# A step size finished in its PSUM bank: one more reader for the bank, one fewer SBUF input for VectorE

## The chip, the cores and the metric

The kernel runs on one core of one Trainium2 chip. The metric is the device time of the launch in microseconds (us), the median of three runs, and lower is better. The core has five engines that each work through their own queue in order: PE (TensorE, matrix multiply), DVE (VectorE), ACT (ScalarE), POOL (GpSimd) and SP (SyncE, which here only issues transfers). Sixteen DMA engines move data between the device memory and the on-chip memory SBUF. Matrix products land in PSUM, a small memory of eight banks; one bank holds 128x512 fp32 values.

## The reference

Four layers work on images of 96 channels and 64x64 pixels, four images in a batch. Layer 0 is a state-space layer: it normalises, projects and convolves the image to an input `u` of 192 channels, and then runs a recurrence over the 4096 pixels, in four directions `k` (by rows and by columns, each forward and back). Layer 1 is a deformable convolution, layer 2 a Fourier mixer with a feed-forward part, layer 3 linear attention with a feed-forward part. Only the input of the recurrence of layer 0 matters for the change:

```python
delta = jax.nn.softplus(dts + delta_bias[None, :, :, None])
def step(h, inp):
    d_t, u_t, b_t, c_t = inp
    dA = jnp.exp(d_t[..., None] * A)
    h = dA * h + (d_t * u_t)[..., None] * b_t[:, :, None, :]
    y = jnp.einsum('bkdn,bkn->bkd', h, c_t)
    return (h, y)
```

The kernel needs the step size `delta` itself (for `dA`) and its product with the convolved input, `delta * u`.

## The kernel before

**The scan.** `Layer0.scan` runs over 1,536 units. A unit is one image, one direction, one of four stretches of 1,024 pixels and eight channels, whose 16 states make 128 partitions. For each unit ScalarE turns the step size into the decay (L1014), TensorE spreads `delta * u` over the states into a PSUM pair `db` (L1020), VectorE multiplies that by the input weights (L1034) and runs the recurrence (L1042), GpSimd multiplies by the output weights (L1051) and TensorE sums the states (L1070). The step sizes come from device memory into `da` tiles, a ring of twelve, with transfers that ScalarE's queue issues (L993).

**Beside the scan** two streams of filler work run. One (`ends`) prepares layer 0 of the next images and then runs layers 2 and 3; the other (`middle`) finishes layer 0 and runs layer 1. All of this is one program: a planner decides while the program is written. Each piece of filler is a generator that yields steps with a planned cost for each engine (`cost(pe=.., dve=.., act=.., pool=..)`), and `pipe` interleaves several such chains (here five, at least two steps apart). A step is put into the program when the planner's clock has room on its engines and the step before it is planned to be over. At the end the program order is fixed for every engine (`in_program_order`).

**Banks.** While the scan runs, all filler shares three PSUM banks (`net.mm`). `holds=1` in a step says that the chain keeps a bank after that step, and a new chain starts only where fewer than three are held. `takes` and `frees` count the tiles of small rings in the same manner.

**The chain that is changed** is `Layer0.steps`, which runs 192 times: six times for each chunk of 512 pixels of each image. A chain covers 128 channels of one direction, or the remaining 64 channels of two. In order it does this:

- TensorE projects into the bank `pd` (L840); ScalarE computes four functions from it (L842 to L846: `ex`, `lw`, `w1`).
- VectorE forms a correction in `w1` (L849), GpSimd subtracts it from `lw` (L851).
- VectorE finishes the step size, `rl = max(pd, 0) + lw`, from PSUM into SBUF (L853), and the bank is free.
- VectorE multiplies `rl` by the convolved input `xa` or `xc`, into `ex`. The four forms are L859 and L860 (halves of 64 partitions), L866 (the input read by columns) and L872.
- SP writes `rl` to device memory (L875, `de`), from where L993 reads it.
- ScalarE and TensorE split `ex` into three bf16 parts (L879 to L889) in another bank, `pr`, and SP writes those out (L894).

L853 and the multiply are two steps of the planner, with a planned VectorE cost of 0.7 us each.

Of the kernel before, what the change touches and what calls it, by code (L numbers as in the profile page):

```python
# [15 lines left out]
ALU = mybir.AluOpType  # L16
# [3 lines left out]
B, C, H, W = 4, 96, 64, 64  # L20
# [162 lines left out]
def cost(pe=0.0, dve=0.0, act=0.0, pool=0.0, **more):  # L183
    return Step((pe, dve, act, pool), **more)


def wait(us=0.0, **more):

    return Step((0.0,) * 4, us, **more)
# [75 lines left out]
class Chain:  # L265
    def __init__(self, steps, ready):
        self.steps, self.ready = steps, ready
        self.done, self.holds, self.new, self.takes = 0, 0, True, []
        self.kind = steps.gi_code


def pipe(net, chains, width, every=0, lane=None, **tiles):
# [5 lines left out]
    while True:  # L278
        if more and len(active) < width:
            steps = next(chains, None)  # L280
            if steps is None:
                more = False
            else:
                active.append(Chain(steps, clock.now()))
                continue
# [269 lines left out]
class Layer0:  # L555
# [267 lines left out]
    def steps(self, b, ks, j, us, dtw, sm, xdbl):  # L823

        net = self.net
        nc = net.nc
        cs = slice(j * CH, (j + 1) * CH)
        tk = f"{b}_{j}_" + "".join(str(k) for k in ks)
        both = len(ks) == 2

        def tile_of(name, bufs):
            return sm.tile([128, CH], F32, name=f"{name}{tk}", tag=name, bufs=bufs)

        yield wait(new=True, takes="ex lw")


        pd = net.mm(f"pd{tk}")
        for i, k in enumerate(ks):
            o, m = (pd[64 * i : 64 * i + 64], slice(128, DI)) if both else (pd, slice(0, 128))
            nc.tensor.matmul(o, lhsT=dtw[:, k, m], rhs=xdbl[k % 2, j], start=True, stop=True)  # L840
        ex = tile_of("ex", 3)
        nc.scalar.activation(ex, pd, AF.Abs)  # L842
        nc.scalar.activation(ex, ex, AF.Exp, scale=-1.0)
        lw, w1 = tile_of("lw", 2), tile_of("w1", 2)
        nc.scalar.activation(lw, ex, AF.Ln, bias=net.one)
        nc.scalar.activation(w1, ex, AF.Identity, bias=net.one)  # L846
        yield cost(pe=2.2 if both else 1.1, act=2.7, holds=1, takes="rl")
        rl = tile_of("rl", 2)
        nc.vector.scalar_tensor_tensor(w1, w1, -1.0, ex, ALU.add, ALU.subtract)  # L849
        yield cost(dve=0.7, holds=1)  # L850
        nc.gpsimd.tensor_sub(lw, lw, w1)  # L851
        yield cost(pool=1.3, holds=1)
        nc.vector.scalar_tensor_tensor(rl, pd, 0.0, lw, ALU.max, ALU.add)  # L853
        yield cost(dve=0.7, frees="lw")
        if both and ks[0] % 2 == ks[1] % 2:
            q, xc = ks[0] % 2, us[2]
            own, far = slice(64 * q, 64 * q + 64), slice(64 - 64 * q, 128 - 64 * q)
            turned = xc.rearrange("p (a b) -> p b a", a=64)
            nc.vector.tensor_mul(ex[own], rl[own], xc[own, cs])  # L859
            nc.vector.tensor_mul(  # L860
                ex[far].rearrange("p (a b) -> p a b", b=64),
                rl[far].rearrange("p (a b) -> p a b", b=64),
                turned[far, j * NR : (j + 1) * NR, :],
            )
        elif not both and ks[0] % 2:
            nc.vector.tensor_mul(  # L866
                ex.rearrange("p (w h) -> p w h", h=H),
                rl.rearrange("p (w h) -> p w h", h=H),
                us[1][:, j * NR : (j + 1) * NR, :],
            )  # L870
        else:
            nc.vector.tensor_mul(ex, rl, us[2 if both else 0][:, cs])  # L872
        parts = ((0, 64, ks[0], 128), (64, 128, ks[1], 128)) if both else ((0, 128, ks[0], 0),)
        for p0, p1, k, c0 in parts:
            nc.sync.dma_start(self.de_d[b][k][c0 : c0 + p1 - p0, cs], rl[p0:p1])  # L875
        yield cost(dve=0.7, takes="du", frees="rl")

        du = sm.tile([128, 3, CH], BF16, name=f"du{tk}", tag="du", bufs=2)
        nc.scalar.copy(du[:, 0, :], ex)  # L879
        yield cost(act=0.6, new=True)  # L880
        pr = net.mm(f"pr{tk}")
        nc.tensor.matmul(pr, lhsT=net.ident, rhs=ex, start=True, stop=False)  # L882
        nc.tensor.matmul(pr, lhsT=self.minus, rhs=du[:, 0, :], start=False, stop=True)
        nc.scalar.copy(du[:, 1, :], pr)
        yield cost(pe=1.5, act=0.6, holds=1, frees="ex")
        nc.tensor.matmul(
            pr, lhsT=self.minus, rhs=du[:, 1, :], start=False, stop=True, skip_group_check=True
        )
        nc.scalar.copy(du[:, 2, :], pr)  # L889
        yield cost(pe=0.4, act=0.6)  # L890
        for p0, p1, k, c0 in parts:
            for p in range(p0, p1, 32):
                dst = self.du_d[b][k, j, (c0 + p - p0) // 32].rearrange("(s c) t -> c s t", s=3)
                nc.sync.dma_start(dst, du[p : p + 32])  # L894
        self.ready.update((b, k, both, j) for k in ks)
        yield wait(frees="du")
# [1044 lines left out]
```

## Time and profile before

| | |
|---|---|
| median of three runs | 8476.31 us (8467.26 to 8499.47) |
| the profiled execution | 8455.38 us, span 8453.6 us |
| VectorE busy | 6826.4 us, 81% of the span |
| TensorE busy | 6424.4 us, 76% |
| GpSimd busy | 5621.2 us, 66% |
| ScalarE busy | 4914.8 us, 58% |
| scan and its multiply, VectorE (L1042, L1034) | 3578.1 and 1865.4 us |
| last chain of step sizes (L889) | starts at 4549.7 us |
| last GpSimd multiply of the scan (L1051) | starts at 7418.8 us |

The busy times of the engines overlap, so they don't add up to the span. A wait that the profile names is read as "instruction that waited <- what ended the wait". The chain of waits is followed back from the last instruction, at each step to what released it. An instruction off this chain can take longer without moving the end, up to some slack that the chain does not show.

### The profile page before, as it was taken

Reading aid. Unit: us, or ns where it says so; the run is one execution under the profiler, and the core shown is the slowest. Engines: PE = TensorE matmul, PEld = TensorE weight load, DVE = VectorE, ACT = ScalarE, POOL = GpSimd, SP = SyncE. Lnnn points to the kernel's source line nnn. Section 1 sums busy time; section 2 is a strip of 40 time slices with the busy share of each in tenths; the row PEclk is TensorE's granted clock in tenths of the full one; section 3 lists DMA queues with packets and bytes.
Section 4 is the critical chain, followed back from the end, with each engine's and each line's share of the span. In section 5 each row is a group of like instructions: output and inputs, shape, how many; then the busy total and the mean of one; then the engine's idle time right before and its main releaser. Section 6 shows DMA issues by size and latency. Waiting matters only on the chain.

```text
span 8453.6 us, 96209 instructions
## 1 busy us (share of the span) xinstructions
PE 6424.4 (76%) x31848; PEld 2772.6 (33%) x31848; DVE 6826.4 (81%) x5122; ACT 4914.8 (58%) x8979; POOL 5621.2 (66%) x4308
## 2 busy tenths in 40 slices
PE   6765787678766777977767889777788777797587
PEld 2211221112222223321222555222455232464273
DVE  2799889987789898779888898898898988838714
ACT  5665566555567777855566677645576876333224
POOL 1566566665568888856578898766798997627700
PEclk8776787678767778977667898786798787898698
DMA  3676678877679888877788999776899897744410
GB/s 98 169 209 186 166 190 214 204 186 188 171 205 241 233 235 220 230 187 198 194 216 233 236 237 245 184 177 175 224 239 235 216 228 188 187 111 138 142 60 17
DMA packets 773926, 1608.27 MB, mean 190 GB/s; under 512 B 264082, under 2 KB 355758, under 8 KB 771223
## 3 DMA queue, kind: packets, MB, share of 16 engines
q10 hardware_dynamic: 244224, 843.17, 39.2%
q1 hardware_dynamic: 455478, 532.37, 24.4%
q0 software_dynamic: 73728, 226.57, 10.1%
q8 instruction: 256, 4.19, 0.2%
q14 instruction: 240, 1.96, 0.1%
HBM read 1345.43 MB, written 256.29 MB: 189 GB/s over the span
## 4 chain that ended last, share of the span: by engine, by line
PE 32%; DVE 26%; DMA 12%; POOL 11%; issue 9%; ACT 8%; SPq 2%; ACTq 1%; DVEq 0%; POOLq 0%
DVE da L1042 12%; POOL da L1051 7%; DVE db L1034 7%; PE pc L763 3%; DMA da<-de 3%; PE py L1070 3%; PE ps L1416 3%; PE f L1510 3%; POOL g L1383 3%; PE pd L1432 2%; PE db L1020 2%; ACT g L1395 2%; ACT da L1014 2%; DMA du<-du 1%; PE h L1551 1%
## 5 line engine op out<-in xcount | busy, mean ns | idle before, releaser
L1051 POOL TENSOR_TENSOR da<-da,bc 128x1024 f32<-128x1024 f32 x1536 | 3664.1, 2387 | 351.6 <-DVE da L1042 233.3
L1042 DVE TENSOR_TENSOR_SCAN da<-da,st,db 128x1024 f32<-128x1024 f32 x1152 | 2701.1, 2345 | 124.1 <-ACT da L1014 12.8
L1034 DVE TENSOR_TENSOR db<-db,bc 128x1024 f32<-128x1024 f32 x1536 | 1865.4, 1214 | 614.7 <-PE db L1020 613.1
L1014 ACT ACTIVATE da<-da,w_al 128x1024 f32<-128x1024 f32 x1536 | 1737.7, 1146 | 405.7 <-DMA da<-de 166.9
L1383 POOL DMA_INDIRECT g<-table,idx x1152 | 1206.8, 1048 | 360.2 <-issue 178.7
L1020 PE MATMUL db<-du,rep 24*128 24x512 bf16 x3072 | 683.7, 450 | 774.4 <-DVE da L1042 729.0
L1070 PE MATMUL py<-da,w_fold 128*32 128x512 f32 x6144 | 1091.8, 784 | 43.6 <-issue 25.2
L1395 ACT ACTIVATE g<-g,wt 128x96 f32<-128x96 f32 x3456 | 964.0, 365 | 107.1 <-DMA g<-table,idx 18.4
L1042 DVE TENSOR_TENSOR_SCAN da<-da,db 128x1024 f32<-128x1024 f32 x384 | 877.0, 2284 | 54.7 <-ACT da L1014 19.6
L1416 PE MATMUL ps<-w_ident,g 128*96 128x128 f32 x3744 | 680.7, 325 | 252.3 <-issue 107.6
L1020 PEld LDWEIGHTS <-rep 24*128 24x128 bf16 x3072 | 147.3, 93 | 1839.2 <-DVE da L1042 1164.6
L851 POOL TENSOR_TENSOR lw<-lw,w 128x512 f32<-128x512 f32 x192 | 244.0, 1271 | 700.5 <-DVE w L849 667.8
L1416 PEld LDWEIGHTS ps<-w_ident,g 128*96 128x96 f32 x3744 | 483.5, 144 | 601.3 <-issue 178.9
L1049 POOL COPY st<-da 128x1 f32<-128x1 f32 x1152 | 232.2, 202 | 674.1 <-DVE da L1042 655.8
L763 PE MATMUL pc<-pad,wc 96*128 96x512 f32 x1152 | 576.3, 636 | 7.0 <-DVE rl L853 5.3
L1424 ACT COPY st<-ps 96x384 f32<-96x384 f32 x384 | 180.2, 472 | 572.3 <-PE ps L1416 533.8
L882 PE MATMUL pr<-ex,w_ident 128*128 128x512 f32 x384 | 311.2, 904 | 125.5 <-DVE ex L866 53.5
L1432 PE MATMUL pd<-st,wdc 96*128 96x256 f32 x1152 | 323.7, 434 | 12.7 <-DVE rl L853 6.0
L763 PEld LDWEIGHTS pc<-pad,wc 96*128 96x128 f32 x1152 | 217.9, 200 | 318.6 <-issue 303.5
L840 PE MATMUL pd<-xd,w_dtw 103*64 103x512 f32 (+1 forms) x512 | 273.4, 799 | 47.0 <-DVE rl L853 15.6
L1070 PEld LDWEIGHTS py<-da,w_fold 128*32 128x32 f32 x6144 | 158.1, 124 | 381.1 <-issue 300.3
L1432 PEld LDWEIGHTS pd<-st,wdc 96*128 96x128 f32 x1152 | 243.2, 219 | 104.2 <-issue 39.5
(259 smaller groups left out, 8631.4 us busy)
## 6 DMA issues: line engine op xcount, KB each, us to landing
da<-de ACTq DMA_DIRECT2D x1536, 512.0 KB
du<-du SPq DMA_DIRECT2D x1536, 96.0 KB
bc<-bcd SPq DMA_DIRECT2D x128, 512.0 KB
y<-yb SPq DMA_DIRECT2D x384, 128.0 KB
de<-rl SPq DMA_DIRECT2D x128, 256.0 KB
m<-in_dft SPq DMA_DIRECT2D x128, 256.0 KB
ad<-y ACTq DMA_DIRECT2D x192, 128.0 KB
table<-pix SPq DMA_DIRECT2D x256, 96.0 KB
```

Of the source, the lines that this page charges most:

```text
L763: nc.tensor.matmul(pp, lhsT=wc[:, q, g * 128 : (g + 1) * 128], rhs=pad[:, r0 + dy : r0 + dy + NR, dx : dx + W], start=(q == 0), stop=(q == 8),
L882: nc.tensor.matmul(pr, lhsT=net.ident, rhs=ex, start=True, stop=False)
L1014: self.net.nc.scalar.activation(u.da, u.da, AF.Exp, scale=self.al[:, a : a + 1])
L1020: self.net.nc.tensor.matmul(db[:, h, :], lhsT=self.rep[64 * u.q + 32 * h : 64 * u.q + 32 * h + 24], rhs=u.du[64 * u.q + 32 * h : 64 * u.q ...
L1034: self.net.nc.vector.tensor_mul(u.db, u.db, u.bc[:, 0, :])
L1042: nc.vector.tensor_tensor_scan(u.along(u.hh), u.along(u.da), u.along(u.db), first, ALU.mult, ALU.add)
L1051: self.net.nc.gpsimd.tensor_mul(u.hh, u.hh, u.bc[:, 1, :])
L1070: nc.tensor.matmul(py[p0 : p0 + 32], lhsT=self.fold[:, u.i, :], rhs=hc[:, h * CH : (h + 1) * CH], start=u.sums["add"] is None and u.i == 0 ...
L1383: nc.gpsimd.indirect_dma_start(out=g[:, k, :], out_offset=None, in_=self.tables[b % 2], in_offset=bass.IndirectOffsetOnAxis(ap=idx[:, n : ...
L1395: nc.scalar.activation(pixel, pixel, AF.Identity, scale=wt[:, n, c : c + 1])
L1416: nc.tensor.matmul(pt[:, k, :], lhsT=g[:, k, c * C : (c + 1) * C], rhs=net.ident, is_transpose=True, start=(c == 0), stop=(c == corners - 1),)
L1432: nc.tensor.matmul(po, lhsT=wdc[:, k, :], rhs=st[:, k, :], start=(k == 0), stop=(k == 8))
```

## The change

VectorE now writes the finished step size back into `pd` in place, and the multiply reads it from there. ScalarE then copies `pd` to `rl`, and SP's transfer of `rl` follows the copy. For the planner the two VectorE instructions are one step of 1.4 us, the bank is held through the copy, the copy is a step of 0.6 us on ScalarE, and an empty step follows the transfer. The tile `rl` is made just ahead of the copy. Nothing else in the program differs; the ring `da` has twelve tiles in both.

```diff
         yield cost(pe=2.2 if both else 1.1, act=2.7, holds=1, takes="rl")
-        rl = tile_of("rl", 2)
         nc.vector.scalar_tensor_tensor(w1, w1, -1.0, ex, ALU.add, ALU.subtract)
         yield cost(dve=0.7, holds=1)
         nc.gpsimd.tensor_sub(lw, lw, w1)
         yield cost(pool=1.3, holds=1)
-        nc.vector.scalar_tensor_tensor(rl, pd, 0.0, lw, ALU.max, ALU.add)
-        yield cost(dve=0.7, frees="lw")
+        nc.vector.scalar_tensor_tensor(pd, pd, 0.0, lw, ALU.max, ALU.add)
         if both and ks[0] % 2 == ks[1] % 2:
             q, xc = ks[0] % 2, us[2]
...
-            nc.vector.tensor_mul(ex[own], rl[own], xc[own, cs])
+            nc.vector.tensor_mul(ex[own], pd[own], xc[own, cs])
             nc.vector.tensor_mul(
                 ex[far].rearrange("p (a b) -> p a b", b=64),
-                rl[far].rearrange("p (a b) -> p a b", b=64),
+                pd[far].rearrange("p (a b) -> p a b", b=64),
...
         elif not both and ks[0] % 2:
             nc.vector.tensor_mul(
                 ex.rearrange("p (w h) -> p w h", h=H),
-                rl.rearrange("p (w h) -> p w h", h=H),
+                pd.rearrange("p (w h) -> p w h", h=H),
...
         else:
-            nc.vector.tensor_mul(ex, rl, us[2 if both else 0][:, cs])
+            nc.vector.tensor_mul(ex, pd, us[2 if both else 0][:, cs])
+        yield cost(dve=1.4, holds=1, frees="lw")
+        rl = tile_of("rl", 2)
+        nc.scalar.copy(rl, pd)
+        yield cost(act=0.6)
         parts = ((0, 64, ks[0], 128), (64, 128, ks[1], 128)) if both else ((0, 128, ks[0], 0),)
         for p0, p1, k, c0 in parts:
             nc.sync.dma_start(self.de_d[b][k][c0 : c0 + p1 - p0, cs], rl[p0:p1])
-        yield cost(dve=0.7, takes="du", frees="rl")
+        yield wait(takes="du", frees="rl")
```

## The prediction

> **What bounds the kernel now.** I read the page's busy shares first, then the windows by stage, the rows of the tiles that change, the waits, and last the chain of waits, which prices each step. The page gives VectorE the largest load, but a chain that changes engine all the time:
>
> ```profile
> PE 6424.4 (76%) x31848; PEld 2772.6 (33%) x31848; DVE 6826.4 (81%) x5122; ACT 4914.8 (58%) x8979; POOL 5621.2 (66%) x4308
> PE 32%; DVE 26%; DMA 12%; POOL 11%; issue 9%; ACT 8%; SPq 2%; ACTq 1%; DVEq 0%; POOLq 0%
> ```
>
> The windows split the span at the last step-size instruction (4540 us), the last scan (7415) and the end of layer 1 (8030):
>
> ```profile
> 182.00:4540.00 4358.00, 3199.78 (x11203) 1016.37 (x11201) 3770.88 (x2615) 2720.84 (x4470) 2936.29 (x2205) 0.76 0.78 203
> 4540.00:7415.00 2875.00, 2309.32 (x14702) 1172.76 (x14702) 2504.63 (x1681) 1795.41 (x3796) 2296.39 (x1775) 0.82 0.86 213
> 7415.00:8030.00 615.00, 441.39 (x2661) 286.03 (x2662) 383.27 (x537) 169.29 (x337) 372.03 (x312) 0.80 0.47 132
> ```
>
> Columns are us, then PE, PEld, DVE, ACT, POOL busy. In the first stage, the only one that runs the changed code, VectorE is busy 3771 of 4358 us (87%), TensorE 73%, GpSimd 67%, ScalarE 62%. Of VectorE's 587 idle us the largest item is 342.9 us in 189 waits for TensorE's L1020, that is, for a TensorE queue that is itself stuck. So no engine bounds the stage alone: VectorE is nearest, and TensorE holds it up.
>
> The rows that change, from the view of tile ex (ns: min/median/max) and, as yardstick, a multiply with one PSUM input (L1613):
>
> ```profile
> L872 DVE TENSOR_TENSOR ex<-rl,xa x64: 680/692/5254, 113.7 to 4537.8; 128x512 f32<-128x512 f32 x64
> L866 DVE TENSOR_TENSOR ex<-rl,xa x64: 1025/1071/3171, 513.8 to 4464.4; 128x512 f32<-128x512 f32 x64
> L872 DVE TENSOR_TENSOR ex<-rl,xc x48: 668/692/4834, 1218.1 to 4495.8; 128x512 f32<-128x512 f32 x48
> L1613 DVE TENSOR_TENSOR tl<-tl,lnb x64: 655/677/684, 4636.9 to 8373.2; 96x512 f32<-96x512 f32 x64
> ```
>
> The minimum of L872 is that of L1613, but its maximum is over seven times its median. The same instruction is sometimes blocked for up to 4.6 us. L866 reads xa by columns and costs 1.03 us even unblocked.
>
> [...] two SBUF inputs reach 5254 ns, one SBUF and one PSUM input never passes 684. [...]
>
> **Part by part**
>
> *Multiplies (L859, L860, L866, L872).* By the groups view they are busy 81.0+53.2 (L872), 102.9 (L866), 26.7 (L860) and 19.7 (L859), 283.5 us in all. With one PSUM input I price them unblocked: 112×0.677 + 64×1.071 + 16×1.042 + 16×0.677 = 172. VectorE loses 112 us of work. How much of it moves the end? The chain's pieces in order of time hold 52.3 (L872, 46 pieces), 50.0 (L866, 35), 20.4 (L860) and 12.4 (L859), 135 us; the saved fraction is 112/283.5 = 0.39, so **−53 us** on the path. Bounds: nothing, to −112 if VectorE alone sets the pace.
>
> *Step size in place (L853).* PSUM in place instead of SBUF out: 678 ns now; the in-place PSUM multiply L1034 is 1208 for 1024 columns[...]. No change. It also stops waiting for the transfer de<-rl (11.2 us, 2 waits); the copy inherits that, so I count 0.
>
> *Copies.* 192 new ScalarE copies, PSUM to SBUF, 128x512; the nearest row, L1081 yb<-py, has a mean of 570 ns: 109 us on ScalarE. Its busy time is on the chain in 8/58 of cases: **+15 us**. Bounds 0 and +109. Queued behind a copy are the decay L1014 and the da<-de issues, twelve tiles deep; VectorE waited for L1014 only 28.9 us in the stage, which is the cover. That ScalarE waits for the multiply is not new: the cast L879 already waits for it (54.8 + 41.2 + 14.6 us); the copy takes that wait over.
>
> *The bank.* pd was free after L853. Now it is held through the multiply (0.68, or 1.07 by columns) and the copy (0.57), 1.3 us longer, on one of three banks. Whoever waits for it is TensorE, and behind that matmul stands L1020, for which VectorE waits:
>
> ```profile
>   PE px L812: 33.7, 14
>   PEld px L812: 31.2, 11
>   PEld pd L840: 20.9, 9
>   PE pd L840: 15.6, 7
> ```
>
> (of L853's view: who waited, us, times). On the chain L853 hands over to a TensorE instruction 21 times: 21×1.3 = **+27 us**. Bounds: 0 if the planner, which knows the hold, finds other work, and 192×1.3 = 250 us of TensorE waiting, at TensorE's share of path to busy (32/76) +105.
>
> *The transfer de<-rl* (L875, on SP) leaves 1.3 us later. SP already stood 509.6 us behind L853 in 124 waits, and behind it wait y<-yb, du<-du and bc<-bcd. The chain goes from L853 to it 5 times: **+6 us**. Its reader da<-de comes only after the three casts, the cover. Counts of SP and POOL instructions don't change.
>
> *The order.* A chain has one step more. In the built program the last step-size instruction of image 3 stands behind scan 951 instead of 892, and the first Fourier add behind 975 instead of 926. No image becomes short of input: image 3 is scanned from 1152. All but a rest is made up later: behind the last scan stand 309 more matmuls, 192 of L1510 (0.068 us), 64 of L1576 (0.146), 48 of L1590 (0.099) and 5 of L1595 (0.56), 30 us of TensorE, and 32 ScalarE copies, 17 us. Image 2, to which they belong, stored its result at 7905 us and image 3 is loaded at 8038, so 133 us of slack cover them; TensorE is 72% busy beside, so I take **+8 us** of 0 to 30.
>
> Sum on the path: −53+15+27+6+8 = +3 us. A path's gain undercounts a relief of the most loaded engine, whose blocked multiplies off the path shorten the next path too. I take −15, a fifth of the way to rival 1. The profiled execution took 8455.4 us (span 8453.6); 8440 on its scale. The median of three runs is 20.9 us higher, so I forecast **8461**: no change, meaning within 0.5% (42 us), about what a measurement of this kernel can tell from none.
>
> **Rivals**
>
> 1. *VectorE sets the pace.* For: 87% busy, and GpSimd waited 521 us for L849, in VectorE's queue. Against: 343 us of its idleness wait for TensorE. All 112 us arrive, the bank waits vanish in the planner: −112+15+8 = −89, 8387.
> 2. *The bank decides; slower.* Three banks, and a later release in a ScalarE queue that runs behind. For: 21 handovers on the chain now. Against: the planner counts the hold. Price 1.3 us per handover: −53+15+6+8 = −24 without the bank, so break-even at 18 handovers, slower by over 42 us from 51, and at the upper bound of +105 it is +81, 8557.
> 3. *No relief.* The blocking does not come from the second SBUF input, and the multiplies stay at a mean of 1.36 us (283.5/208). Against: L1613's maximum. +15+27+6+8 = +56, 8532.
>
> **Chances.** Forecast 0.38 (8434 to 8518); rival 1 and partial versions of it 0.33; rival 2 0.22 and rival 3 0.07. The 8-in-10 range, 8375 to 8560, leaves out little beyond the far ends of 1 and 2.
>
> **What would show it.** Multiplies with a maximum under 0.72 us (1.1 by columns), about 172 us in all; 192 copies of 0.57 us; TensorE's waits for the copy in place of those for L853, at 21 handovers or so on the chain; last scan within 40 us of 7415; image 2 stored before image 3 loads. A mean multiply above 1.2 us, over 50 handovers, or a last scan before 7350 would make the forecast wrong.

## The result, and the profile after

The changed kernel took 8452.7 us (median of 20 runs), the kernel before 8482.9 beside it: a ratio of 0.997, with a 95% interval of 0.9956 to 0.9983. The forecast was 8461 us and no change within 0.5%. Both hold; the gain of 0.3% is real but small. Two later sets gave 0.9949 (0.9932 to 0.9967) and 0.9965 (0.9947 to 0.9982).

The two profiled executions do not show this gain: after's took 8460.7 us, a little above its median, and before's 8455.4, below its own. So the profiles are read for where time went, and the runs for how much.

The page of the changed kernel (busy times, then the chain by engine):

```profile
PE 6423.3 (76%) x31810; PEld 2788.5 (33%) x31848; DVE 6748.3 (80%) x5122; ACT 5005.0 (59%) x9171; POOL 5580.3 (66%) x4308
PE 32%; DVE 28%; DMA 11%; POOL 10%; ACT 9%; issue 8%; ACTq 1%; SPq 1%; DVEq 0%; another core or an unknown queue 0%; POOLq 0%
```

VectorE is busy 78 us less and ScalarE 90 us more, but VectorE's share of the chain rose by two points. The windows, cut within some 10 us of the events of before (end of the step sizes, of the scan, of layer 1; columns us, then PE, PEld, DVE, ACT, POOL):

```profile
182.00:4747.00 4565.00, 3331.22 (x11912) 1078.78 (x11948) 3900.47 (x2738) 2953.03 (x5008) 3118.71 (x2381) 0.76 0.80 206
4747.00:7410.00 2663.00, 2127.56 (x13427) 1079.81 (x13430) 2306.60 (x1560) 1634.55 (x3415) 2081.61 (x1600) 0.82 0.84 208
7410.00:8043.00 633.00, 496.39 (x3216) 338.18 (x3208) 374.04 (x535) 186.69 (x368) 363.76 (x311) 0.81 0.47 134
```

The step sizes now end at 4747 us instead of 4550, the scan at 7410 instead of 7419. The tail, from the last GpSimd multiply of the scan to image 3's load, is 633 us instead of 619. The first stage is longer because the new order spreads its chains over more units of the scan (953 scans start before its end, where 896 did), not because a unit takes longer: the scan as a whole ends 9 us earlier.

The multiplies, in the view of tile ex (ns: min/median/max):

```profile
L870 DVE TENSOR_TENSOR ex<-pd,xa x64: 690/691/692, 112.8 to 4738.7; 128x512 f32<-128x512 f32 x64
L864 DVE TENSOR_TENSOR ex<-pd,xa x64: 1005/1036/1104, 522.0 to 4690.8; 128x512 f32<-128x512 f32 x64
L870 DVE TENSOR_TENSOR ex<-pd,xc x48: 690/691/692, 1201.8 to 4701.8; 128x512 f32<-128x512 f32 x48
```

The maxima of 5254, 3171 and 4834 ns are gone. All five groups add up to 66.5 + 44.2 + 33.2 + 16.6 + 11.0 = 171.5 us, where 283.5 stood before.

That is 112 us less, but VectorE as a whole is busy only 78 us less. The largest part of the difference is the chain's first VectorE instruction, which still has two SBUF inputs. The groups of before and after (busy us, mean ns after the bar):

```profile
L849 DVE SCALAR_TENSOR_TENSOR w<-w,ex 128x512 f32<-128x512 f32 x192 | 156.2, 813 | 79.3 <-ACT w L846 78.4 <-DMA bcd<-xd 0.9
```

```profile
L848 DVE SCALAR_TENSOR_TENSOR w<-w,ex 128x512 f32<-128x512 f32 x192 | 178.7, 931 | 99.3 <-ACT w L846 98.3 <-DMA da<-de 0.9
```

It is blocked for 22 us more now. GpSimd is busy 41 us less as well, 28 of them in its multiply of the scan (3664.1 to 3636.1 us).

The view of the copy's line: its durations, and who waited for it (us, times).

```profile
L873 ACT COPY rl<-pd x192: 560/586/603, 115.8 to 4739.9; 128x512 f32<-128x512 f32 x192
...
  PEld ps L1418: 28.2, 11
  PEld pr L884: 17.4, 11
  PE ps L1418: 17.3, 10
  PEld pd L840: 16.8, 5
```

The copy itself stands behind the multiply in this program: the same view gives it 53.6 us in 28 waits for L864, 48.6 in 33 for L870 and 6.6 in 5 for L858, about the 110.6 us that the cast waited before. TensorE does wait behind the copy now. On the chain, though, the copy hands over to TensorE only 10 times; L853 did so 21 times.

### The profile page after: what moved, and what is told of

Read it like the earlier page. It is cut to its first block, busy times and chain, and to the rows that moved or that the text cites. A ratio compares the mean times of both kernels' runs of the same rounds, so it can differ in the third digit from the quotient of the medians.

```text
span 8458.9 us, 96090 instructions
## 1 busy us (share of the span) xinstructions
PE 6423.3 (76%) x31810; PEld 2788.5 (33%) x31848; DVE 6748.3 (80%) x5122; ACT 5005.0 (59%) x9171; POOL 5580.3 (66%) x4308
## 4 chain that ended last, share of the span: by engine, by line
PE 32%; DVE 28%; DMA 11%; POOL 10%; ACT 9%; issue 8%; ACTq 1%; SPq 1%; DVEq 0%; another core or an unknown queue 0%; POOLq 0%
DVE da L1044 13%; POOL da L1053 7%; DVE db L1036 7%; PE pc L763 4%; PE ps L1418 3%; PE py L1072 3%; PE f L1512 3%; ACT g L1397 2%; PE pd L1434 2%; PE db L1022 2%; ACT da L1016 2%; POOL g L1385 2%; DMA da<-de 1%; DMA du<-du 1%; PE h L1553 1%
## 5 line engine op out<-in xcount | busy, mean ns | idle before, releaser
L1053 POOL TENSOR_TENSOR da<-da,bc 128x1024 f32<-128x1024 f32 x1536 | 3636.1, 2369 | 286.4 <-DVE da L1044 166.4
L1418 PEld LDWEIGHTS ps<-w_ident,g 128*96 128x96 f32 x3744 | 502.1, 149 | 532.0 <-ACT g L1397 151.2
L886 ACT CAST du<-pr 128x512 bf16<-128x512 f32 x192 | 111.6, 581 | 275.2 <-PE pr L885 190.1
L1521 ACT COPY d<-f 128x512 f32<-128x512 f32 x192 | 111.6, 583 | 273.3 <-PE f L1512 272.9
```

The lines of the kernel that those rows point to most:

```text
L1053: self.net.nc.gpsimd.tensor_mul(u.hh, u.hh, u.bc[:, 1, :])
L1418: nc.tensor.matmul(pt[:, k, :], lhsT=g[:, k, c * C : (c + 1) * C], rhs=net.ident, is_transpose=True, start=(c == 0), stop=(c == corners - 1),)
```

## The experiments

Four kernels ran per set, each set on one chip. Kernels are compared only within a set, because the chips differ: the kernel before took 8500.7 us in the first set, 8477.9 in the second and 8477.7 in the third.

### First set: the order, the relief, the copies, VectorE's load

**e1_plan_only** keeps the instructions of the kernel before and takes over the planner's steps of the changed one. Its order is that of the changed kernel on every engine, without the copies.

```diff
         nc.vector.scalar_tensor_tensor(rl, pd, 0.0, lw, ALU.max, ALU.add)
-        yield cost(dve=0.7, frees="lw")
...
             nc.vector.tensor_mul(ex, rl, us[2 if both else 0][:, cs])
+        yield cost(dve=1.4, holds=1, frees="lw")
+        yield cost(act=0.6)
...
-        yield cost(dve=0.7, takes="du", frees="rl")
+        yield wait(takes="du", frees="rl")
```

> The instructions of the kernel before in exactly the order of the changed one on every engine: the step size goes to SBUF, the multiply has two SBUF inputs, there is no ScalarE copy; only the planner is told of the longer hold and the copy's 0.6 us. It prices the order alone. Theory A (the prediction: half of the 112 us of relief reaches the end, bank waits and copies take most of it back, the order costs about 8 us): ratio to the kernel before 1.001, within 0.998 to 1.004. Theory B (VectorE sets the pace, all 112 us arrive, and the order is what takes 70 us of them back): 1.006 to 1.010. Theory C (the chip's own bank waits decide, and the planner's order in fact avoids them): below 0.998.

Measured: 1.0102 (1.0085 to 1.012). The order alone costs 1%, 87 us, some ten times the 8 us of the prediction. That is theory B's number, on this chip.

**e2_no_copy** is the changed kernel without the copies. What SP stores is a constant tile, `self.flat`, so its transfer no longer waits for any engine's result.

```diff
-        rl = tile_of("rl", 2)
-        nc.scalar.copy(rl, pd)
+        rl = self.flat
         yield cost(act=0.6)
```

> The changed kernel without the 192 ScalarE copies; the stored step size is a constant tile written once, so the recurrence runs on wrong step sizes. Same order, the bank is free on the chip after the multiply. It prices the copy and the bank time that belongs to it. Theory A: the copy costs 15 us on the path and 12 us of the bank term (0.57 of 1.3 us), so 27 us less than the changed kernel, ratio to the kernel before 0.994. Theory B (ScalarE is not on the path at all): 0.996 to 0.998, like the changed kernel. Theory C (the late release behind ScalarE's queue decides): 0.989 or less.

Measured: 1.0009 (0.9994 to 1.0024). Its value lay outside every theory's range; each had been reckoned from 0.997 for the changed kernel, which was not in this set. What the set does give is e1 against e2, the same order with and without the blocked multiplies: 1.0102 to 1.0009, which is 0.92% or 79 us (give or take 20) for the relief. Two other things differ between the two and are in this figure: in e2 the bank is held through the multiply, and the transfer waits for nothing.

**e3_copy_twice** makes each copy twice (`nc.scalar.copy(rl, pd)` repeated).

> The changed kernel with each ScalarE copy made twice, same order: 109 us more on ScalarE and the bank 0.57 us longer. Theory A: 27 us more than the changed kernel, ratio to the kernel before about 1.000. Theory B: 0.996 to 0.998, like the changed kernel. Theory C: over 1.003, and growing faster than the first copy did. If ScalarE's busy time came through whole it would be 1.010.

Measured: 1.0031 (1.0017 to 1.0046). Against e2 without any copy, two copies cost 0.22%, 19 us (give or take 18) for 224 us of ScalarE work. One copy is worth some 9 us, with the bank time and the wait of the transfer that belong to it. The ratio itself is in theory C's range, but only because the whole set lies higher than was assumed; the step that C expected between the kernels is missing.

**e4_multiply_twice** makes each multiply twice.

```diff
+        for _ in range(2):
             if both and ks[0] % 2 == ks[1] % 2:
...
```

> The changed kernel with each multiply made twice, same order: 171 us more VectorE work, unblocked, with one PSUM input, and the bank about 0.8 us longer. It measures how much of VectorE's load reaches the end. Theory A: at VectorE's share of path to busy time (28/80) 60 us, and up to 15 for the bank: ratio to the kernel before about 1.006 (1.003 to 1.009). Theory B (all of it arrives): 1.017. Theory C: as A, since the bank time counts and not the load, 1.002 to 1.006.

Measured: 1.0099 (1.0074 to 1.0124). Against e3 (two copies, single multiply) that is 0.68% or 58 us, against e2 0.90% or 76 us; the changed kernel, with one copy, should lie between. So 171 us more on VectorE cost 58 to 76 us, each give or take some 25: a third to under a half comes through, near the 60 to 75 us of theory A. VectorE does not set the pace alone.

### Second set: what in the order costs, and the kernels once more

**e5_plan_no_hold** is e1 without the hold: `yield cost(dve=1.4, frees="lw")`.

> As e1_plan_only (instructions of the kernel before, no copy, multiply with two SBUF inputs), but the planner is no longer told of the longer bank hold; the joined VectorE step, the planned 0.6 us of ScalarE and the empty step stay. It splits the order's cost. New theory (D: all of the relief is nearly worth its VectorE time, and the order takes most of it back): most of the order's 1.0% comes from the hold, because it is the bank that makes the chains of step sizes slower; ratio to the kernel before 1.002 to 1.005. Rival (E: the joined step and the longer chain do it): 1.008 to 1.011.

Measured: 1.0116 (1.0097 to 1.0136). The cost is there without the hold, so telling the planner of the bank is not needed for it. The number is at the upper end of rival E's range: the joined step, the planned ScalarE time and the extra empty step are enough. Which of the three does it was not tested.

**e6_changed_again** and **e7_before_again** are the two kernels themselves.

> The changed kernel once more, beside the others, so that e1 to e4 can be set against it. Theory D: 0.997, as measured before; then e1 says that order and relief are +1.0% and -1.3%. Rival (the chip of e1 to e4 made every kernel of that order slower): the ratio moves to 1.000 or above, and the order is dearer on some chips than on others.

> The kernel before once more, as a kernel of this set, for a profile of the same chip and for the width of a comparison: ratio 1.000, within 0.002. After the last scan it should need about 620 us to the end of layer 1, as in its first profile, if the 667 to 682 us of e1 to e4 come from their order; about 660 if they come from the chip.

Measured: 0.9949 (0.9932 to 0.9967), and 0.9993 (0.998 to 1.0006) for the kernel before against itself. From the last GpSimd multiply of the scan to image 3's load e7 needed 616 us and e6 629, where e1 to e4 had needed 667 to 683. So the order alone does not make those long tails; e9, with the order of e1, needed 633 in the third set. Whether the kernel before has them on the chip of the first set is not known, since it was not profiled there.

**e8_two_steps** gives the changed instructions another plan.

```diff
         nc.vector.scalar_tensor_tensor(pd, pd, 0.0, lw, ALU.max, ALU.add)
+        yield cost(dve=0.7, holds=1, frees="lw")
...
-        yield cost(dve=1.4, holds=1, frees="lw")
+        yield cost(dve=0.7, holds=1)
         rl = tile_of("rl", 2)
         nc.scalar.copy(rl, pd)
-        yield cost(act=0.6)
...
-        yield wait(takes="du", frees="rl")
+        yield cost(act=0.6, takes="du", frees="rl")
```

> The changed kernel with another plan: step size and multiply are two VectorE steps of 0.7 us again, both with the bank held, and the transfer is issued in the copy's step. All instructions are those of the changed kernel. In its order the step sizes of image 3 end at scan 941 instead of 951 (892 before) and 144 fewer matmuls stand behind the last scan. Theory D: part of the order's cost comes back, ratio to the kernel before 0.992 to 0.996. Theory A: as the changed kernel, 0.997.

Measured: 1.0017 (1.0006 to 1.0029), 0.7% slower than the changed kernel beside it. The expectation was wrong: this order looks closer to that of the kernel before by both of its marks, and is slower. How early the step sizes end and how much stands behind the last scan did not foretell the time here.

### Third set: the whole account on one chip

**e9_plan_only_2**, **e10_no_copy_2** and **e11_changed_2** are e1, e2 and the changed kernel side by side.

> e1_plan_only once more, now beside the changed kernel on one chip: the order alone, without relief and without copies. Theory D (the order costs about 1%, the relief gives over 1% at that order, the copies cost next to nothing): ratio to the kernel before 1.009 to 1.013. Rival F (the 1.0% was a matter of that chip): 1.000 to 1.006.

> e2_no_copy once more (constant step sizes stored, so the recurrence runs on wrong ones), beside the changed kernel and e9. e9 to e10 is the relief alone in one order, e10 to the changed kernel the 192 copies alone. Theory D: 79 us below e9, as on the chip of e1 and e2, and 5 to 15 us below the changed kernel: ratio 0.994 to 1.001. Rival A (relief 53 us on the path, copies and their bank time 27): 53 us below e9 and 27 below the changed kernel.

> The changed kernel, third time. Ratio 0.995 to 0.997 if the chip is like the first and the third; about 1.002 if it is like that of e1 to e4, where e2 and e3 put it by interpolation. Between it and e10 stands the price of the copies: 10 us (theory D) or 27 (A).

| step | ratio to before | the step alone |
|---|---|---|
| the order (e9) | 1.0056 (1.0038 to 1.0075) | +47 us |
| plus the relief, with the bank held through the multiply (e10) | 0.9978 (0.9965 to 0.999) | -66 us |
| plus the copies, with the rest of the hold and the transfer behind them (e11, the changed kernel) | 0.9965 (0.9947 to 0.9982) | -11 us, within the intervals of nothing |

The last column is the difference of ratios times 8478 us, give or take 16 to 19 us. In e10 the transfer of the constant tile waits for nothing, where SP stood 301 us behind L853 in e9; so the split between the last two rows is less sure than their sum, -77 us from e9 to e11. The order's ratio lies in the range of rival F: the order is dear on this chip too, but at little more than half of the figure of the first, so theory D's 1% seems to have been partly a matter of the chip. The relief is 66 us where it was 79, between D and A, and the copies are not to be seen. These groups of e9 and then of e10 show the relief (busy us, mean ns after the bar):

```profile
L865 DVE TENSOR_TENSOR ex<-rl,xa 128x512 f32<-128x512 f32 x64 | 115.2, 1800 | 2.2
L871 DVE TENSOR_TENSOR ex<-rl,xa 128x512 f32<-128x512 f32 x64 | 95.3, 1490 | 2.3
```

```profile
L866 DVE TENSOR_TENSOR ex<-pd,xa 128x512 f32<-128x512 f32 x64 | 66.6, 1040 | 2.2
L872 DVE TENSOR_TENSOR ex<-pd,xa 128x512 f32<-128x512 f32 x64 | 44.2, 691 | 2.2
```

All five groups add up to 319.7 us in e9 and 171.6 in e10. In the new order the blocked multiplies would have cost 320 us, not the 283.5 of the kernel before: they are blocked more there. Of 148 us less, 66 reach the end. A part of the rest shows up as waiting: VectorE's largest wait in the first stage, for TensorE's spread of the next unit (us, times, longest), is longer in e10, the second line, than in e9, the first.

```profile
DVE db L1035 <- PE db L1021: 380.3, 191, 25.9
```

```profile
DVE db L1037 <- PE db L1023: 436.9, 205, 27.2
```

**e12_second_relief** takes the other instruction with two SBUF inputs out of the chain (L848, mean 870 ns in e11). ScalarE makes the first term with a constant `net.minus_one`, which is set up elsewhere.

```diff
         nc.scalar.activation(w1, ex, AF.Identity, bias=net.one)
-        yield cost(pe=2.2 if both else 1.1, act=2.7, holds=1, takes="rl")
-        nc.vector.scalar_tensor_tensor(w1, w1, -1.0, ex, ALU.add, ALU.subtract)
+        nc.scalar.activation(w1, w1, AF.Identity, bias=net.minus_one)
+        yield cost(pe=2.2 if both else 1.1, act=3.4, holds=1, takes="rl")
+        nc.vector.scalar_tensor_tensor(pd, pd, 0.0, ex, ALU.max, ALU.add)
         yield cost(dve=0.7, holds=1)
         nc.gpsimd.tensor_sub(lw, lw, w1)
         yield cost(pool=1.3, holds=1)
-        nc.vector.scalar_tensor_tensor(pd, pd, 0.0, lw, ALU.max, ALU.add)
+        nc.vector.tensor_add(pd, pd, lw)
```

> A version that goes one step further: the correction's first term is made by a fifth ScalarE instruction (0.7 us), VectorE adds ex to max(pd, 0) in the bank, GpSimd subtracts without waiting for VectorE, and VectorE adds the result into the bank. So no VectorE instruction of the chain has two SBUF inputs any more; the one it replaces took 931 ns in the mean where 682 is unblocked, 48 us in all. Theory D: 0.57 of 48 us gained, about 10 us lost on ScalarE: 17 us below the changed kernel, 20 more if GpSimd's wait for VectorE counts; but the order moves again (120 more matmuls behind the last scan), so anything from 0.990 to 1.000 is open. Theory A: as the changed kernel.

Measured: 1.012 (1.0095 to 1.0145), outside every expectation. The blocking did go, as the group of the new instruction shows, but VectorE's largest wait in the first stage grew. The lines are the group of e12, then the wait in the waits view of e12, then the same wait in that of e11 (us, times, longest):

```profile
L851 DVE SCALAR_TENSOR_TENSOR pd<-pd,ex 128x512 f32<-128x512 f32 x192 | 132.0, 688 | 93.9 <-ACT ex L845 93.9
```

```profile
DVE db L1039 <- PE db L1025: 540.9, 233, 24.6
```

```profile
DVE db L1036 <- PE db L1022: 423.4, 200, 30.5
```

VectorE saved 35 us on this line (167.1 to 132.0) and waited 117 us more for TensorE's spread of the next unit. Whether the added ScalarE work or the order it came with made TensorE late is not settled; only both together were run. The runs of e12 also had a lower granted TensorE clock, 0.7823 in the mean against 0.7907 for the kernel before. Among runs of one kernel of this set 0.001 less clock went with some 4.6 us more, so by an estimate from these figures 38 of e12's 99 us go along with the clock; which is cause and which effect is not shown. No version ran faster than the changed kernel.

## Why the prediction was right, and which of its terms were not

**The blocking: right in kind and size.** Multiplies were to have a maximum under 0.72 us (1.1 by columns) and 172 us in all; they have 694 ns, 1104 ns and 171.5 us. That a second SBUF input brings the blocking had been inferred from two maxima, 5254 and 684 ns; the multiplies after bear it out. On the chain of waits they held 135 us before and hold 81 after, 54 less where the forecast had 53. In one order the relief is worth 66 us (third set) and 79 (first). It is more than 53 mainly because the new order would have blocked more: about half of the time saved on VectorE comes through, 0.45 of 148 us in the third set, where the step took 53/112 = 0.47. Two things the step left out: the blocking of L849 grew by 22 us, of which 13 came with the relief itself (158.8 us in e9, 172.0 in e10), and GpSimd was relieved as well. How much of the gain is GpSimd's was not separated. The step size in place took about as long as before: 686 ns in the median (L852) against 678.

**The copies and the bank: too dear.** The runs split these terms in another way than the forecast did. A copy with its 0.57 us of the bank's 1.3 and with the transfer was forecast at 15 + 12 + 6 = 33 us; it measured some 9 in the first set and nothing above the noise in the third. The copy's own time on the chain is 13.7 us, close to the 15. What was too dear is the bank: 21 handovers were forecast, and the chain of the changed kernel has 10. The hold through the multiply, the other 15 us of the bank's 27, was never run alone and is inside the figure of the relief. Rival 2 is out: the kernel is not slower, and two copies keep the bank longer still and cost 19 us.

**The order: the term that failed.** It was taken as +8 us of 0 to 30, read off the work behind the last scan. The third set puts it at +47 us (1.0056), the first at +87 (1.0102 of 8501 us). The tail gave only 13 of it in the profile of the changed kernel. Most lies within the scan: in e9 the last GpSimd multiply of the scan starts at 7477.5 us, 59 later than in the profile of before, and 54 later than in e7. Some of that is the extra blocking (36 us of VectorE, half of which would count). Some may go with the clock: the runs of e9 had 0.7876 granted in the mean and those of before 0.7907, which is 14 us by the estimate above, again without showing which is the cause. The rest is not traced to one wait and stays open.

**The sum.** The path gave +3 us and I took -15; the third set's terms give 47 - 66 - 11 = -30. In the runs' split the forecast was 8 for the order, -53 + 15 = -38 for the relief with the hold through the multiply, and 33 for the copies. So the order was underpriced by 39 us, and the other two came out 28 and 44 us better. The total was close because these errors cancelled, which is luck; that the blocking goes and about half of it counts was foreseen. Rival 1 (all of VectorE's relief arrives) is refuted by e4 and by the 66 of 148 us from e9 to e10. Rival 3 is refuted by the multiplies. One reading was off: the 342.9 us of VectorE's waits for L1020 leave out the first 18 us of the stage; the stage from 182 us on has 375.3 in 192 waits, which speaks the same way.

**The slack.** Image 2 was to be stored before image 3 loads; it was, at 7980 us against 8043, but the slack shrank from 133 us to 63.

## What to carry to other kernels

In the profiles shown here VectorE instructions with one PSUM input in place of an SBUF input lost their blocking, with GpSimd busy beside them for 68% of the first stage (3118.7 of 4565.0 us in after): the multiplies by rows have a mean of 691 ns in after and in e10, where they had 1266 before and 1490 in e9, and L851 of e12 has 688, where the instruction it replaces has 870 in e11. Look at once for the next instruction with two SBUF inputs, since a part of the blocking can move there, as 22 us did to L849 here. Of the time saved about half (66 of 148 us in the third set) reached the end in this kernel, whose chain keeps changing engine. Where a planner fixes the order, price the new order as an item of its own, with a kernel that has the new order and the old instructions: here it took back 47 of 77 us in one set and about the whole gain of the relief, 87 against 79 us, in another. A further relief of the same kind is not sure to pay: with what it added on ScalarE and the order that it brought, e12 was 129 us slower than the changed kernel, where its line saved 35.

## What the runs showed of the hardware that was not expected

A blocked multiply does not always get its turn between two GpSimd instructions that follow each other. In e9 the longest one took 9.06 us. The timelines of VectorE and then of GpSimd (start, us):

```profile
3907.22 9.06 DVE L871 TENSOR_TENSOR ex<-rl,xa 128x512 f32<-128x512 f32 x1
```

```profile
3906.43 9.30 POOL L1052 TENSOR_TENSOR da<-da,bc 128x1024 f32<-128x1024 f32 x4
```

GpSimd ran four multiplies back to back, to 3915.73, and VectorE's ended 0.55 us later. The 5.25 us multiply of the kernel before lies within four such multiplies in a row too (9.25 us from 3836.07): it began just before the second ended and waited out the third and fourth. But elsewhere in e9 VectorE did get in between two of them:

```profile
1474.40 1.63 DVE L871 TENSOR_TENSOR ex<-rl,xa 128x512 f32<-128x512 f32 x1
```

```profile
1473.08 5.16 POOL L1052 TENSOR_TENSOR da<-da,bc 128x1024 f32<-128x1024 f32 x2
```

The first GpSimd multiply ended at 1475.48 and VectorE's at 1476.02, again some 0.55 us later, while the second took 2.81 us, where the four of 9.30 us took 2.33 each in the mean. Which of the two went first when GpSimd had another instruction ready differed between the two cases, and what decides it is not shown. An instruction with one PSUM and one SBUF input was not held up in such a row: in the kernel before, L853 took 0.67 us from 3839.92, while the four GpSimd multiplies ran that held up the one of 5.25 us; its median over all 192 is 678 ns.

The by-column multiply costs 1036 ns with one PSUM input and 1071 with none, against 691 by rows: most of the extra comes with the column read and not with the second SBUF input.
